# Weight sums by accumulating DMAs, and plain products in the first block alone: an RWKV layer and a feed-forward layer on one core

## The chip, the core and the metric

The kernel runs on one core of one Trainium2 chip. TensorE (PE) multiplies, VectorE (DVE) and ScalarE (ACT) do elementwise work, GpSimd (POOL) and SyncE (SP) issue DMAs. The metric is the device time of one execution in microseconds; smaller is better. Before the change it is 1259.82 us, the median of three runs from 1258.47 to 1259.84 us.

## What is computed

Input is x, 2048 tokens of 512 numbers, in float32 throughout. Two layers follow one another, each behind a layer norm and with a residual. Cut to what matters:

```python
# layer 1 (RWKV): h is a norm of x, hh is h shifted by one token
k = (h * tm_mk + hh * (1 - tm_mk)) @ Wk.T
v = (h * tm_mv + hh * (1 - tm_mv)) @ Wv.T
r = (h * tm_mr + hh * (1 - tm_mr)) @ Wr.T
x = x + sigmoid(r) * wkv(k, v) @ Wo.T            # "time mix"
kk = (h * cm_mk + hh * (1 - cm_mk)) @ Wkey.T     # h: a second norm, "channel mix"
kv = silu(kk) @ Wval.T
sr = sigmoid((h * cm_mr + hh * (1 - cm_mr)) @ Wcr.T)
x = x + sr * kv
# layer 2: h is a norm of x
gate, up = split(h @ w_gate_up.T)
out = (silu(gate) * up) @ w_down.T
x = x + out
```

Wk, Wv, Wr, Wo and Wcr are 512 x 512; Wkey, Wval, gate, up and down are four such blocks each.

## The kernel before

The 2048 tokens are cut into four blocks of 512 (`NB` = 4). Every product of a block is a 512 x 512 x 512 matrix product, or four of them. Most are computed by a Strassen-Winograd scheme, `unit` (L508): each matrix is cut into 2 x 2 quarters of 256, and seven products of quarters take the place of eight. A product of quarters is four matmul instructions of 128x128 by 128x256, each of which the profile shows as two records. The scheme needs four sums of the weight's quarters (S1 to S4, with S1 = A21+A22, S2 = S1-A11, S3 = A11-A21, S4 = A12-S2) and four of the operand's (T1 to T4). `plain_unit` (L619) is the ordinary product, 32 matmul instructions instead of 28, with no sums. The down product of the last layer applies the scheme twice, so that its weight needs sums of sums.

**Weight sums.** `prepare` (L140) makes the four sums of one weight. It loads the four quarters (256 KB each) on GpSimd's queue, adds them on VectorE in four tensor_tensor instructions, and stores the four sums in DRAM, again on GpSimd's queue. There are 32 such blocks: 21 weights, four for the first level of the down weight (`("d", k)`), seven for the second (`("dd", q)`). `weight` and `down_weight` (L164, L170) load a quarter or a sum into a ring of 12 tiles on SP's queue when a product needs it; for a sum, `need_sums` (L275) first makes sure that its instructions have been put out. The first nine blocks use four tiles of the large pool `q`, the others four of the six tiles of the pool `prep`.

**The order of the work.** PE, DVE and ACT execute exactly in the order in which the Python code issues instructions (`manual_schedule`, L1221). GpSimd's and SP's DMAs are placed by the framework's scheduler. The code interleaves by a plan: after each eight or so records of PE, `tick` (L287) grants VectorE a share of that time (`STEP` 1.72 us), and lets background work (norms, mixes, sums of operands) put out instructions until the share is spent. The preparation of weights is metered by `credit`: it grows by `credit[1]` at each tick, and a step of a `prepare` may go when it is at least 1. After a block's loads, `WAIT` = 5 ticks go by before its first addition. `paced` (L127) ties a load to the last matmul issued, so that it doesn't run ahead.

**The sequence.** Block 0's k product comes first, in halves (`first_block`, L729); then r and v of block 0, k of block 1, the output product of block 0, r and v of block 1. The loop over the blocks (L1248) then runs for each block the gate product (WCR), the next block's output product, four up products (WKEY), the down product (WVAL), and the time mix of the block after next. Layer 2 follows (L1286): gate and up products (WG, WU) in four groups, then the twice-cut down product. `PLAIN` = 2 says that blocks 0 and 1 use `plain_unit` for the products of WK, WV, WR and WO.

**Evictions.** `unit` copies partial results from PSUM on ACT (`snapshot`, L542) and adds others on DVE (`add`, L546). Behind that, each product's `sink` applies the nonlinear function on ACT or DVE.

Of the kernel before, what the change touches and what calls it, by code (L numbers as in the profile page):

```python
# [9 lines left out]
F32 = mybir.dt.float32  # L10
AF = mybir.ActivationFunctionType
ALU = mybir.AluOpType
# [3 lines left out]
P = 128  # L16
# [3 lines left out]
NT = TB // P  # L20
HB = TB // 2
EPS = 1e-5
PLAIN = 2
WAIT = 5
STEP = 1.72
SHARE = 0.88
WARM = 44
# [31 lines left out]
def rwkv_ffn_kernel(  # L59
# [29 lines left out]
    def q_tile(name):  # L89
        return pools["q"].tile([P, 2, HB], F32, tag="q", name=name)  # L90
# [30 lines left out]
    for q in (A11, A12, A22, S1, S2, S3, S4):  # L121
        sources["dd", q] = [wd[q, k] if q < 4 else sums["d", k][q - 4] for k in range(4)]
        sums["dd", q] = scratch(f"dd{q}", 4)

    latest = []

# [10 lines left out]
            raw.append(t)  # L137
        return raw

    def prepare(n, own):  # L140

        raw = []
        for k in range(4):
            t = prep.tile([P, 2, HB], F32, tag="raw", name="raw") if own else q_tile("q")
            paced(nc.gpsimd.dma_start(flat(t), sources[n][k]))
            raw.append(t)
        yield 1
        a11, a12, a22, a21 = raw
        for k, o, i0, i1, op in (
            (0, a22, a21, a22, ALU.add),  # L150
            (2, a21, a11, a21, ALU.subtract),
            (1, a11, a22, a11, ALU.subtract),
            (3, a12, a12, a11, ALU.subtract),
        ):
            tt(o, i0, i1, op)
            nc.gpsimd.dma_start(sums[n][k], flat(o))
            yield

    def ring(src):
        t = wring.tile([P, 2, HB], F32, tag="w", name="w")  # L160
# [81 lines left out]
    preps = deque()  # L242
    credit = [0.0, 0.0]

    def prep_one():
        item = preps[0]
        if item[1] > 0:
            return False
        try:
            if next(item[2]) is not None:  # L250
                item[1] = WAIT
        except StopIteration:
            preps.popleft()
            finished.add(("sums", item[0]))
            if len(preps) > 1 and item[3] > 1:
                begin(preps[1])
            elif preps:
                begin(preps[0])
        return True

    def begin(item):
        if not item[4]:
            item[4] = True
            next(item[2])
            item[1] = WAIT

    def prepare_all(ns, own, depth):
        empty = not preps
        for n in ns:
            preps.append([n, 0, prepare(n, own), depth, False])  # L270
        if empty:
            for item in list(preps)[:depth]:
                begin(item)

    def need_sums(n):  # L275
        while ("sums", n) not in finished:
            begin(preps[0])
            preps[0][1] = 0
            prep_one()

    def due():
        for item in put_off:
# [2 lines left out]
            put_off.popleft()[1]()  # L285

    def tick(length=STEP):  # L287
        for item in preps:
            item[1] -= 1
        slack[0] = max(min(slack[0] + SHARE * length - spent[0], 2.5), -2.5)  # L290
        spent[0] = 0.0
        credit[0] = min(credit[0] + credit[1], 2.0)
        while slack[0] > 0 and (hot or background or preps):
            go = False
            if preps and credit[0] >= 1 and prep_one():
                credit[0] -= 1
                go = True
            elif hot or background:
                go = run_one(False)
            slack[0] -= spent[0]  # L300
            spent[0] = 0.0
            if not go:
                break
# [117 lines left out]
    def shifted_norm(s, h, hT, g, b):  # L421
# [10 lines left out]
        nc.vector.tensor_copy(carry[s], hT[:, :, TB : TB + 1])  # L432
        cost(0)

    def sums_of(B):

        for o, i0, i1 in (T1, B12, B11), (T2, B22, T1), (T4, B21, T2), (T3, B22, B12):
            tt(B[o], B[i0], B[i1], ALU.subtract)
            yield

    live_ops = [0]

# [286 lines left out]
    def first_block():  # L729


        xb = xin.pop(0)
        hT = htp.tile([P, NC, TB + 1], F32, tag="hT", name="hT_a")
        hTs[0, "a"] = hT
        h = tok_tile("h")
        m, B = op_tile("mix")
        ops[0, "k"] = B
        finished.add((0, "k"))
        mhalf = const.tile([P, 4], F32, name="mhalf")
        nc.vector.memset(mhalf, -0.5)  # L740
        cols = []

        def normed(j):
            mv = small.tile([P, 2, 2], F32, tag="mv", name="mv")
            yield from moments(xb[:, 2 * j : 2 * j + 2, :], mv)
            var = small.tile([P, 4], F32, tag="var2", name="var2")
            affine(var, mv)
            two = small.tile([P, 4], F32, tag="two", name="two")
            nc.gpsimd.tensor_tensor(two, var, mhalf, ALU.pow)
            yield  # L750
            for t in range(2):
                cols.append((mv[:, t, 0:1], two[:, t : t + 1]))
                ts(
                    h[:, 2 * j + t, :],
                    xb[:, 2 * j + t, :],
                    mv[:, t, 0:1],
                    two[:, 2 + t : 3 + t],
                    ALU.subtract,
                    ALU.mult,
                )  # L760
                yield

        def mixed(j, other):
            at = slice(j * HB, (j + 1) * HB)
            by_one = slice(j * HB + 1, (j + 1) * HB + 1)
            for c in range(NC):
                pt = bank()
                for t in range(2):
                    nc.tensor.transpose(
                        pt[:, 0, t * P : (t + 1) * P],  # L770
                        h[:, 2 * j + t, c * P : (c + 1) * P],
                        ident,
                    )
                nc.scalar.activation(
                    hT[:, c, by_one],
                    pt[:, 0, :],
                    AF.Identity,
                    bias=vcol(LN1B, c),
                    scale=vcol(LN1G, c),
                )  # L780
                d = m[:, 2 * (c // 2) + j, c % 2, :]
                nc.scalar.activation(d, hT[:, c, at], AF.Copy, scale=onem[:, 0, c : c + 1])  # L782
                stt(d, hT[:, c, by_one], vcol(MK, c), d, ALU.mult, ALU.add)
                next(other, None)

        one, two = normed(0), normed(1)
        for _ in range(3):
            next(one)
        next(two)
        for _ in one:  # L790
            pass
        constants()
        nc.vector.tensor_copy(hT[:, :, 0:1], carry["a"])
        next(two)
        next(two)
        mixed(0, two)
        for _ in two:
            pass

        def second():  # L800
            mixed(1, iter(()))
            tails[0] = residual(0, xb, cols)
            nc.vector.tensor_copy(carry["a"], hT[:, :, TB : TB + 1])
            finished.add("norm0")
            slack[0] = spent[0] = 0.0

        return second

# [255 lines left out]
    def quarter_sums(b, n):  # L1064
        x = quarter_operand(b, n)
        asked.add((b, n))

        def run():
            for o, i0, i1 in (T1, B12, B11), (T2, B22, T1), (T4, B21, T2), ("T3", B22, B12):
                tt(x[o], x[i0], x[i1], ALU.subtract)  # L1070
                yield

        urgent((b, "quarters", n), run())

# [139 lines left out]

    early = [WCR] + [WKEY + g for g in range(4)] + [WVAL + g for g in range(4)]
    late = [n + g for g in range(4) for n in (WG, WU)] + [("dd", A11)]
    late += [("d", k) for k in range(4)] + [("dd", q) for q in (S4, S2, A12, S1, S3, A22)]

    ctx.enter_context(  # L1221
        tc.manual_schedule(
# [4 lines left out]
    for n in "rv":  # L1227
        push_mix(0, n, time_mix(0, n))
    push_residual(0)
    credit[1] = 0.5  # L1230
    k_unit(0)
    prepare_all(early, False, 2)
    xin[1] = load_x(1)
    push("norm1", time_norm(1))
    for n in "krv":
# [8 lines left out]
    push_mix(0, "ck", channel_mix(0, "ck"))  # L1244
    r_unit(1)
    v_unit(1)
    prepare_all([WK, WR, WV, WO] + late, True, 1)
    for b in range(NB):  # L1248
        nxt = b + 2 < NB
        if nxt:  # L1250
# [9 lines left out]
        for g in range(4):  # L1260
            up_unit(b, g)
            if b == 1 and g == 0:
                credit[1] = 0.55
            if g == 0:
                if nxt:
                    push_mix(b + 2, "k", time_mix(b + 2, "k"))
                    push_residual(b + 2)
                    push_mix(b + 2, "r", time_mix(b + 2, "r"))
                if b + 1 < NB:
                    push(f"normb{b + 1}", channel_norm(b + 1))  # L1270
                if nxt:
                    push_mix(b + 2, "v", time_mix(b + 2, "v"))
                if b + 1 < NB:
                    push_mix(b + 1, "cr", channel_mix(b + 1, "cr"))
                    push_mix(b + 1, "ck", channel_mix(b + 1, "ck"))
# [3 lines left out]
        if nxt:  # L1279
            for n, u in (("k", k_unit), ("r", r_unit), ("v", v_unit)):  # L1280
                u(b + 2)
    while preps:
        need_sums(preps[-1][0])
    mixes.close()
    last_room()
    for b in range(NB):  # L1286
# [85 lines left out]
```

## Time and profile before

| | |
|---|---|
| median of three runs | 1259.82 us |
| the profiled execution | 1260.03 us |
| its span, from the first to the last instruction | 1258.2 us |
| granted TensorE clock, mean | 0.997 |
| matmul records on PE | 6572 |
| matmul records of `plain_unit` (L640) | 512 |
| DMAs on SP's queue: w from sum / in_w / dd / d / in_wd | 304 / 256 / 112 / 48 / 36 |
| the same, median us from issue to landing | 3.3 / 3.3 / 3.5 / 3.4 / 3.6 |
| bytes read from and written to HBM | 245.39 MB, 41.94 MB |
| DMA engines, mean rate over the span | 229 GB/s |
| ACT activation with silu, 128x512 (L924) | 631 ns each |
| ACT copy from PSUM, 128x512 (L544) | 584 ns each |

The span is what the profile divides; the execution's own time lies 1.8 us above it. A row of the groups of instructions names the line, the engine, the operation, the tiles it writes and reads, their shape, how often it occurs, the busy time and the mean of one, and then how long the engine sat idle just before it and what ended that. Most elementwise rows carry L363, since one helper (`tt`) issues them all, so they are told apart by their tiles: raw and q are weight quarters, mix, s, t and zT operands, u partial results. In a row of a stretch of time each engine has its busy time and count, and the last three columns are the granted clock, the busy share of the 16 DMA engines, and GB/s.

### The profile page before, as it was taken

To read this page: it belongs to the slowest core of one execution; us is meant where nothing else is said; L and a number is where in the kernel's file an instruction comes from. 1 tells how busy PE (TensorE), PEld (TensorE's weight loads), DVE (VectorE), ACT (ScalarE), POOL (GpSimd) and SP (SyncE) were. 2 spreads that over 40 slices of the span, in tenths; PEclk is the share of its full clock that TensorE was granted. 3 is DMA by queue.
4 is the path that set the end of the run, shared out by engine and by line. 5 is a ranking of instruction groups with operands and counts; after the bars stand their busy time and mean duration, and the time that the engine had idled before them with its cause. 6 is when DMAs were issued, how large, how long until landed. Compare 5 with 4: busy or idle time off the path is not lost.

```text
span 1258.2 us, 18321 instructions
## 1 busy us (share of the span) xinstructions
PE 1240.0 (99%) x6572; PEld 1110.7 (88%) x6572; DVE 777.4 (62%) x1416; ACT 369.0 (29%) x687; POOL 151.3 (12%) x276
## 2 busy tenths in 40 slices
PE   9999999999999999999999999999999999999998
PEld 8888888878888888888888888998899988998898
DVE  5756577567786576743473466565766566564476
ACT  6533252252533433302320222112221223112211
POOL 2222211211222212122220000000000000000000
PEclk9999999999999999999999999999999999999999
DMA  6666777887787777789875654795459854785575
GB/s 205 222 209 232 242 242 255 258 269 243 246 264 243 268 251 244 233 279 332 273 253 183 221 154 144 242 337 175 143 169 301 284 154 146 231 291 165 152 220 199
DMA packets 137960, 288.55 MB, mean 229 GB/s; under 512 B 17296, under 2 KB 18320, under 8 KB 136848
## 3 DMA queue, kind: packets, MB, share of 16 engines
q1 hardware_dynamic: 115424, 215.53, 54.9%
q0 software_dynamic: 21440, 70.27, 15.6%
q10 hardware_dynamic: 1008, 1.59, 0.3%
q8 instruction: 53, 0.87, 0.3%
q14 instruction: 35, 0.29, 0.1%
HBM read 245.39 MB, written 41.94 MB: 228 GB/s over the span
## 4 chain that ended last, share of the span: by engine, by line
PE 93%; ACT 3%; DVE 2%; DMA 1%; issue 1%; POOL 0%; DVEq 0%
PE ps L527 71%; PE ps L1126 14%; PE ps L640 6%; PE ps L414 2%; ACT mix L465 1%; DMA raw<-in_w 1%; DVE u L363 0%; DMA w<-in_w 0%; DVE mix L371 0%; DMA x<-in_x 0%; ACT r L835 0%; ACT e L840 0%; DVE e L371 0%; ACT x L701 0%; ACT mix L782 0%
## 5 line engine op out<-in xcount | busy, mean ns | idle before, releaser
L527 PE MATMUL ps<-zT,w 128*128 128x256 f32 x1792 | 391.4, 379 | 0.0
L527 PEld LDWEIGHTS ps<-zT,w 128*128 128x128 f32 x1792 | 338.7, 190 | 45.4
L527 PE MATMUL ps<-mix,w 128*128 128x256 f32 x1232 | 275.9, 383 | 6.0 <-ACT s L544 6.0
L527 PEld LDWEIGHTS ps<-mix,w 128*128 128x128 f32 x1232 | 235.8, 192 | 40.1 <-ACT s L544 7.6
L363 DVE TENSOR_TENSOR u<-ps,u 128x512 f32<-128x512 f32 x128 | 88.5, 692 | 149.2 <-PE ps L527 144.8
L544 ACT COPY u<-ps 128x512 f32<-128x512 f32 x128 | 74.8, 584 | 319.4 <-PE ps L527 319.4
L527 PE MATMUL ps<-w,s 128*128 128x256 f32 x512 | 114.3, 379 | 0.0
L527 PEld LDWEIGHTS ps<-w,s 128*128 128x128 f32 x512 | 97.0, 190 | 13.1
L1126 PE MATMUL ps<-w,hid 128*128 128x128 f32 x832 | 104.7, 275 | 0.4 <-ACT r L1138 0.4
L1126 PEld LDWEIGHTS ps<-w,hid 128*128 128x128 f32 x832 | 99.5, 192 | 1.1 <-ACT r L1138 0.5
L527 PE MATMUL ps<-w,t 128*128 128x256 f32 x432 | 96.5, 379 | 3.1 <-issue 1.8
L527 PEld LDWEIGHTS ps<-w,t 128*128 128x128 f32 x432 | 81.8, 190 | 14.8 <-issue 2.2
L1126 PE MATMUL ps<-w,quads 128*128 128x128 f32 x704 | 89.5, 276 | 0.4 <-ACT r L1138 0.4
L363 DVE TENSOR_TENSOR s<-ps,s 128x512 f32<-128x512 f32 x64 | 44.2, 690 | 69.0 <-PE ps L527 54.0
L1126 PEld LDWEIGHTS ps<-w,quads 128*128 128x128 f32 x704 | 84.3, 192 | 1.1 <-ACT r L1138 0.5
L640 PE MATMUL ps<-mix,w 128*128 128x256 f32 x384 | 83.8, 379 | 1.1 <-DVE mix L371 1.1
L640 PEld LDWEIGHTS ps<-mix,w 128*128 128x128 f32 x384 | 72.6, 190 | 11.1 <-DVE mix L371 1.5
L363 DVE TENSOR_TENSOR u<-u,u 128x512 f32<-128x512 f32 x64 | 44.0, 688 | 51.7 <-ACT u L544 51.7
L1138 ACT COPY r<-ps 128x128 f32<-128x128 f32 x112 | 29.6, 264 | 142.7 <-PE ps L1126 142.7
L363 DVE TENSOR_TENSOR raw<-raw 128x512 f32<-128x512 f32 x92 | 63.2, 687 | 12.0 <-DMA raw<-d 4.5
L1208 POOL DMA_DIRECT2D out<-resid x12 | 8.6, 717 | 469.9 <-DVE resid L363 469.9
L363 DVE TENSOR_TENSOR hid<-hid 128x512 f32<-128x512 f32 x84 | 56.6, 687 | 1.1
(127 smaller groups left out, 1179.4 us busy)
## 6 DMA issues: line engine op xcount, KB each, us to landing
w<-sum SPq DMA_DIRECT2D x304, 256.0 KB, 3.3
w<-in_w SPq DMA_DIRECT2D x256, 256.0 KB, 3.3
w<-dd SPq DMA_DIRECT2D x112, 256.0 KB, 3.5
raw<-in_w POOLq DMA_DIRECT2D x48, 256.0 KB, 4.9
sum<-raw POOLq DMA_DIRECT2D x48, 256.0 KB, 3.9
w<-d SPq DMA_DIRECT2D x48, 256.0 KB, 3.4
q<-in_w POOLq DMA_DIRECT2D x36, 256.0 KB, 6.0
sum<-q POOLq DMA_DIRECT2D x36, 256.0 KB, 3.5
```

What stands on the lines that cost most here:

```text
L363: nc.vector.tensor_tensor(out, a, b, op)
L414: nc.tensor.transpose(flat[:, t * P : (t + 1) * P], h[:, t, c * P : (c + 1) * P], ident)
L465: nc.scalar.activation(dst(c), hT[:, c, 0:TB].rearrange("p (j t) -> p j t", j=2), AF.Copy, scale=onem[:, row - MK, c : c + 1],)
L527: mm = nc.tensor.matmul(pz[:, m, :], lhsT=lhsT, rhs=rhs, start=first and g == 0 and m == 0 and k == 0, stop=g == last and k == 1, skip_gro ...
L544: nc.scalar.copy(tmp[name], acc["z"])
L640: mm = nc.tensor.matmul(acc[i, j][:, m, :], lhsT=act[:, k, lo] if by_token else wg[:, k, lo], rhs=wg[:, k, :] if by_token else act[:, k, : ...
L1126: mm = nc.tensor.matmul(dst, lhsT=x[k][:, g, :], rhs=wt[:, g, :], start=first and g == 0, stop=g == 3, skip_group_check=True,)
L1138: nc.scalar.copy(st["r"][:, m, n * P : (n + 1) * P], st["z"])
L1208: eng.dma_start(out_t[b][:, 2 * j : 2 * j + 2, i * HB : (i + 1) * HB], rs[b][:, 2 * j : 2 * j + 2, i * HB : (i + 1) * HB],)
```

## The change

It does three things.

1. `prepare` no longer adds on VectorE. It takes two tiles instead of four, loads A21 and A22 into them, multiplies both by -1 on ACT, and then makes each sum by a DMA on GpSimd's queue that adds its source to the tile (`accum_op`): t2 = -A22, plus t1 (-A21) gives -S1; t1 plus A11 gives S3; t2 plus A11 gives -S2; t2 plus A12 gives S4. After each, the tile is stored. Only additions occur, so S1 and S2 change their sign, and the operand sums T1, T2 and T4 are formed to match (`sums_in`): T2 by a scalar_tensor_tensor in the place of a tensor_tensor.
2. The two calls of `prepare_all` with their own depths become one queue of 32 blocks, in the order WK, WR, WV, WCR, WO, WKEY, WVAL, WG and WU, d, dd. Up to `DEPTH` = 3 are under way at once (`flying`), in turns. The first three begin in `second`, halfway through the first product. Steps of the preparation no longer count against VectorE's share in `tick`; they go at 2.4 a tick, and at 1.0 from the second block's first up product on, where it was 0.5 and then 0.55.
3. `PLAIN` is 1: in block 1 the products of WK, WR, WV and WO are units of seven products.

```diff
-PLAIN = 2
+PLAIN = 1
 WAIT = 5
+DEPTH = 3
...
+    AFTER = {("dd", q): [("d", k) for k in range(4)] for q in (S1, S2, S3, S4)}
...
-    def prepare(n, own):
-
-        raw = []
-        for k in range(4):
-            t = prep.tile([P, 2, HB], F32, tag="raw", name="raw") if own else q_tile("q")
-            paced(nc.gpsimd.dma_start(flat(t), sources[n][k]))
-            raw.append(t)
+    def prepare(n):
+
+        a11, a12, a22, a21 = sources[n]
+        t1, t2 = prep_tile(), prep_tile()
+        for t, src in (t1, a21), (t2, a22):
+            paced(nc.gpsimd.dma_start(t, src))
         yield 1
-        a11, a12, a22, a21 = raw
-        for k, o, i0, i1, op in (
-            (0, a22, a21, a22, ALU.add),
-            (2, a21, a11, a21, ALU.subtract),
-            (1, a11, a22, a11, ALU.subtract),
-            (3, a12, a12, a11, ALU.subtract),
-        ):
-            tt(o, i0, i1, op)
-            nc.gpsimd.dma_start(sums[n][k], flat(o))
+        for t in t1, t2:
+            nc.scalar.activation(t, t, AF.Copy, scale=-1.0)
             yield
+
+        def add(t, src, k):
+            nc.gpsimd.dma_start(t, src, accum_op=ALU.add)
+            yield
+            nc.gpsimd.dma_start(sums[n][k], t)
+            yield
+
+        yield from add(t2, t1, 0)
+        yield from add(t1, a11, 2)
+        yield from add(t2, a11, 1)
+        yield from add(t2, a12, 3)
...
+    flying = []
+
+    def take():
+
+        while preps and len(flying) < DEPTH:
+            n = preps[0]
+            if n in AFTER and any(("sums", k) not in finished for k in AFTER[n]):
+                return
+            preps.popleft()
+            gen = prepare(n)
+            next(gen)
+            flying.append([n, WAIT, gen])
+
+    def prep_step(item):
+        flying.remove(item)
+        try:
+            next(item[2])
+            flying.append(item)
+        except StopIteration:
+            finished.add(("sums", item[0]))
...
     def prep_one():
+        take()
+        for item in flying:
+            if item[1] <= 0:
+                prep_step(item)
+                return True
+        return False
...
-        credit[0] = min(credit[0] + credit[1], 2.0)
-        while slack[0] > 0 and (hot or background or preps):
-            go = False
-            if preps and credit[0] >= 1 and prep_one():
-                credit[0] -= 1
-                go = True
-            elif hot or background:
-                go = run_one(False)
+        credit[0] = min(credit[0] + credit[1], 4.0)
+        while credit[0] >= 1 and prep_one():
+            credit[0] -= 1
+        while slack[0] > 0 and (hot or background):
+            go = run_one(False)
...
+    def sums_in(B, t3):
+        tt(B[T1], B[B11], B[B12], ALU.subtract)
+        yield
+        stt(B[T2], B[B22], -1.0, B[T1], ALU.mult, ALU.subtract)
+        yield
+        tt(B[T4], B[B21], B[T2], ALU.add)
+        yield
+        tt(B[t3], B[B22], B[B12], ALU.subtract)
+        yield
...
             slack[0] = spent[0] = 0.0
+            take()
+            credit[1] = 2.4
...
-    credit[1] = 0.5
     k_unit(0)
-    prepare_all(early, False, 2)
...
-    prepare_all([WK, WR, WV, WO] + late, True, 1)
...
             if b == 1 and g == 0:
-                credit[1] = 0.55
+                credit[1] = 1.0
```

More of the change, by code (lines that the diff above doesn't have):

```diff
@@ L138, in raw_quarters, with prep_tile @@
         return raw
-    def prepare(n, own):
-        raw = []
-        for k in range(4):
-            t = prep.tile([P, 2, HB], F32, tag="raw", name="raw") if own else q_tile("q")
-            paced(nc.gpsimd.dma_start(flat(t), sources[n][k]))
-            raw.append(t)
-        yield 1
-        a11, a12, a22, a21 = raw
-        for k, o, i0, i1, op in (
-            (0, a22, a21, a22, ALU.add),
-            (2, a21, a11, a21, ALU.subtract),
-            (1, a11, a22, a11, ALU.subtract),
-            (3, a12, a12, a11, ALU.subtract),
-        ):
-            tt(o, i0, i1, op)
-            nc.gpsimd.dma_start(sums[n][k], flat(o))
-            yield
+    def prepare(n):
[3 more added lines that the diff above has]
+            paced(nc.gpsimd.dma_start(t, src))
+        yield 1
+        for t in t1, t2:
+            nc.scalar.activation(t, t, AF.Copy, scale=-1.0)
+            yield
+        def add(t, src, k):
[7 more added lines that the diff above has]
+        yield from add(t2, a12, 3)
+    def prep_tile():
+        return prep.tile([P, 2 * HB], F32, tag="raw", name="raw")
     def ring(src):
@@ L243, in rwkv_ffn_kernel @@
     credit = [0.0, 0.0]
-    def prep_one():
[L246 to L273, printed above, removed]
+    flying = []
[15 more added lines that the diff above has]
+            finished.add(("sums", item[0]))
+    def prep_one():
+        take()
[4 more added lines that the diff above has]
+        return False
     def need_sums(n):
         while ("sums", n) not in finished:
-            begin(preps[0])
-            preps[0][1] = 0
-            prep_one()
+            take()
+            prep_step(next((item for item in flying if item[0] == n), flying[0]))
     def due():
@@ L287, in tick @@
     def tick(length=STEP):
-        for item in preps:
+        for item in flying:
             item[1] -= 1
@@ L433, in shifted_norm @@
         cost(0)
+    def sums_in(B, t3):
[7 more added lines that the diff above has]
+        yield
     def sums_of(B):
-        for o, i0, i1 in (T1, B12, B11), (T2, B22, T1), (T4, B21, T2), (T3, B22, B12):
-            tt(B[o], B[i0], B[i1], ALU.subtract)
-            yield
+        yield from sums_in(B, T3)
     live_ops = [0]
@@ L805, in second @@
             slack[0] = spent[0] = 0.0
+            take()
+            credit[1] = 2.4
         return second
@@ L1068, in run @@
         def run():
-            for o, i0, i1 in (T1, B12, B11), (T2, B22, T1), (T4, B21, T2), ("T3", B22, B12):
-                tt(x[o], x[i0], x[i1], ALU.subtract)
-                yield
+            yield from sums_in(x, "T3")
         urgent((b, "quarters", n), run())
@@ L1213, in ffn_down @@
         down_product(b, sink, final)
-    early = [WCR] + [WKEY + g for g in range(4)] + [WVAL + g for g in range(4)]
-    late = [n + g for g in range(4) for n in (WG, WU)] + [("dd", A11)]
-    late += [("d", k) for k in range(4)] + [("dd", q) for q in (S4, S2, A12, S1, S3, A22)]
+    preps.extend([WK, WR, WV, WCR, WO] + [n + g for n in (WKEY, WVAL) for g in range(4)])
+    preps.extend(n + g for g in range(4) for n in (WG, WU))
+    preps.extend([("d", k) for k in range(4)])
+    preps.extend(("dd", q) for q in (A11, A12, A22, S1, S2, S3, S4))
     ctx.enter_context(
@@ L1281, in rwkv_ffn_kernel @@
                 u(b + 2)
-    while preps:
-        need_sums(preps[-1][0])
+    while preps or flying:
+        need_sums(preps[-1] if preps else flying[-1][0])
     mixes.close()
```

## The prediction

> **What bounds the kernel now.** I read the busy shares first, then the chain of waits, then PE's own list of waits, and last the DMA views, because the change lives on GpSimd's queue.
>
> ```profile
> PE 1240.0 (99%) x6572; PEld 1110.7 (88%) x6572; DVE 777.4 (62%) x1416; ACT 369.0 (29%) x687; POOL 151.3 (12%) x276
> PE 93%; ACT 3%; DVE 2%; DMA 1%; issue 1%; POOL 0%; DVEq 0%
> 157.18 56.98 PE ps L527 x264
> PE ps L527 <- ACT s L544: 6.0, 3, 2.3
> PE ps L414 <- DVE h L367: 1.4, 2, 0.7
> ```
>
> PE is busy for 1240.0 of 1258.2 us and makes 93% of the chain. The third line is one piece of that chain: 264 matmul records without a gap in 56.98 us, so 0.2158 us a record. The fourth and fifth are the largest waits that PE shows after the start, and they come to a few microseconds. Two things only can move the time: fewer records on PE, or something that makes PE wait. VectorE's 62% holds nothing up.
>
> The DMA side has to be read as well:
>
> ```profile
> q0 software_dynamic: 21440, 70.27, 15.6%
> ...
> raw<-in_w POOLq DMA_DIRECT2D x48, 256.0 KB, 4.9
> sum<-raw POOLq DMA_DIRECT2D x48, 256.0 KB, 3.9
> ...
> raw<-in_wd POOLq DMA_DIRECT2D x28, 256.0 KB, 5.1
> ```
> ```profile
> L145 POOL DMA_DIRECT2D raw<-in_w x48 | 26.1, 549 | 44.2 <-PE ps L527 36.7 <-DMA sum<-raw 5.0 <-issue 2.5
> ...
> L363 DVE TENSOR_TENSOR raw<-raw 128x512 f32<-128x512 f32 x92 | 63.2, 687 | 12.0 <-DMA raw<-d 4.5 <-DMA raw<-in_w 4.4 <-issue 1.1
> ```
> ```profile
> 20.00:302.00 282.00, 277.02 (x1305) 243.07 (x1304) 190.68 (x367) 115.25 (x195) 63.90 (x116) 0.99 0.73 239
> ```
> ```profile
> GB/s 0 0 0 0 0 27 75 20 75 259 416 396 410 410 389 403 403 406 373 394 316 328 410 382 376 430 376 396 403 410 382 382 403 362 376 369 369 376 410 403
> ```
>
> A load on POOL's queue lands 4.9 us after its issue, a store 3.9 us, and the issue itself takes 0.55 us. GpSimd's queue used 15.6% of 16 engines for 268 DMAs: 0.156 x 1258.2 / 268 = 0.73 us of all sixteen for each 256 KB. In the window from 20 to 302 us the DMA engines were 73% busy at 239 GB/s. The last line is the first 12 us, where nothing but loads runs: about 395 GB/s is the most that this trace sustains.
>
> **The change, part by part.**
>
> *Fewer matmuls.* With PLAIN at 1, the four units K, R, V and O of block 1 (each 32 matmuls, 64 records) become units of seven products (28 matmuls, 56 records). That takes 4 x 8 = 32 records from PE: 32 x 0.2158 = **-6.9 us**, all of it on the path. The built order agrees: 3,388 matmuls stand where 3,404 stood. The other engines' share has cover: SP gets 3 x 4 = 12 more loads of 256 KB, ACT 12 more copies (0.58 us each), VectorE 32 more adds; all three are far below PE's load.
>
> *Sums leave VectorE.* 32 blocks x 4 tensor_tensor x 0.687 = 88 us go, 32 x 0.69 = 22 us come with the new units. VectorE loses 66 us of 777, worth nothing while PE is the bound. The operand sums (one scalar_tensor_tensor for one tensor_tensor, 0.69 both) cost nothing. But the planner (tick) no longer charges the sums to VectorE, so the norm of block 1 is put earlier: PE's four-way transposes at L414 now stand after 56 instead of 68 plain matmuls, 24 records or 5.2 us sooner. PE waited 1.4 us there for h. I put **+4 us**, from 0 to +7.
>
> *Negations on ACT.* 64 activations of 128x512, nearest row the plain 630 ns one: 40 us on an engine with 29% load. Their length is hidden. Their **wait** is not: each waits for a load on POOL's queue, and behind it in ACT's order stand the copies (L544) that empty PSUM. If the load is late, ACT stops, then PE. Before, this wait was VectorE's, with 11 us in all in the row of L363.
>
> *The pace.* This is the step that decides. In the order before, the 32 blocks' sums are spread from PE's 40 us to its 637 us (the 32 last stores stand that far apart): 19 us a block. In the new order the 320 DMAs stand between 20 and 302 us of PE's work, **8.8 us a block**, because credit is 2.4 per tick until the second channel mix. SP's loads wait for the stores too, but the ring of 12 tiles is 12 x 8 x 0.2158 = 20.7 us deep, and the first use of the gate weights is only at 666 us; ACT's wait comes first.
>
> Can POOL's queue do it in 8.8? For one block the tile t2 goes through load, negation, add, store, add, store, add, store, each waiting for the landing of the one before. With a for an add's landing: 4.9 + 0.7 + 3a + 3 x 3.9 = 17.3 + 3a, shared by three blocks under way. The add is not in this trace. From below: a store's uncrowded minimum in the list of sum is 2.3 us, and one as fast as that would make the chain shorter than 8.8. From above: the rule below, or 6.0, the q loads. **The nearest row** is the load, same queue, same bytes, HBM to SBUF (96 of 128 adds read HBM): a = 4.9. The chain is then 32 us, 10.7 a block, if the three overlapped perfectly. They don't: POOL issues in order, and an issue that waits holds the other blocks back. Walking down POOL's order as built (an issue starts when the one before is issued and what it needs has landed): loads at 0 to 2.8, adds at 6.2, 11.6 and 12.2, the three first stores 11.1, 16.5 and 17.1, and so on; the third block's last store lands at 42.3. Carried on to the end of the order it is 443 us, **13.8 a block**; the last block's second load lands at 410.
>
> From 20 us on, that is 430 us. The negation of this tile stands in ACT's order behind a copy that PE reaches at about 290 us unstalled (gate unit of block 1). PE does not stop the moment ACT does: a unit takes three PSUM banks (z, v, x) of eight in its 12 us, so PE can run on for between 0 and some 25 us; I take 15. **430 - 290 - 15 = +125 us** of stall, spread in steps of 2 to 20 us from about 70 us on.
>
> *A rule against it.* The row says that an add costs what a load costs. The Trainium skill, "Collectives: The Full Stack", section "The bandwidth ceiling: the fold count and why AG ≠ RS ≠ AR", says that an add in the DMA engines reads two sources, two read descriptors a chunk, and so runs at half the rate of a copy. No run here shows an add yet. By it an add holds the sixteen engines for 2 x 0.73 us, so a = 5.6 as an estimate: the walk gives 15.0 a block, its last load 32 us later, stall +157. I take the row, since a quarter of the adds read SBUF and the queue's fixed latency makes most of 4.9, and keep the rule for the range.
>
> *Issue cost* of an add: 0.55, at most double; POOL waits for landings most of the time, so it adds some 5 us at most; taken as 0.
>
> **Sum**, against the profiled execution's span of 1258.2: -6.9 + 4 + 125 = 1380; that execution took 1260.0, 0.2 above the median of 1259.8. With the terms that overlap (the wait of the norm lies ahead of the first stall and gives POOL time), I say **1378 us**.
>
> **Rivals.**
>
> 1. *POOL's chain is late, adds near a load's landing*: 1340 to 1415, 1378 likeliest. For it: 8.8 against 10.7 even with perfect overlap. Chance 0.52.
>
> 2. *The DMA engines are the bound.* In the fast stretch SP moves 43 MB, POOL's plain DMAs 49 and the adds 34: 125 MB, at 395 GB/s 317 us for what is ordered into 282; with the second read of the adds 159 MB, 402 us. Bandwidth alone gives +35 to +120, but on top, landings then grow over 4.9 and 3.9, which were measured at 239 to 262 GB/s. With a = 6.4 the walk gives 16.4 a block: stall about +195, 1450. Chance 0.20. Against it: a stalled PE asks for fewer weights.
>
> 3. *Adds land sooner than loads*, a near 3.9: 12.3 a block, last load 45 us earlier, stall +80; with shorter stores still less. 1275 to 1340, say 1320. Chance 0.17.
>
> 4. *The cover holds: faster.* If an add and a store both land in about 2.6 us, the walk gives 8.5 a block, POOL keeps to the order, ACT never waits, and the 32 records come off: 1259.8 - 6.9 = 1253, or 1257 with the wait at the transposes. The point from which it decides: an add and a store together under about 5.5 us, while the stores alone are at 3.9. Chance 0.08, and 0.03 for a result within the bound of no change. That the records do not go is excluded by the built order.
>
> **How the numbers follow.** Changes under 0.2% (2.5 us) can't be told from none. Slower: 0.52 + 0.20 + 0.17 = 0.89; faster 0.08; same 0.03. The range 1285 to 1470 leaves out rival 4 and no change (0.11), the lowest of 3 and the tail of 2.
>
> **What would show it.** Right: POOL's DMAs up to the last weight sum end past 400 us instead of near 300; PE's waits for ACT total over 80 us between 70 and 450 us; ACT's negations wait for "DMA raw"; PE after that stretch is as before. The landing of raw<-raw and raw<-in_w adds settles a. Wrong: adds that land in under 3 us, or negations that don't wait. If PE's records are fewer by other than 32, the first step fails; if PE waits for "w<-sum" rather than for ACT, the place of the wait does.

## The result, and the profile after

The changed kernel takes **1455.72 us** (median, from 1453.33 to 1457.02), the kernel before 1259.83 us in the same comparison: a ratio of 1.1551, 95% interval 1.1529 to 1.1573. It is 196 us slower. The profiled execution took 1455.54 us, its span is 1453.6 us.

The first fence is the page of the changed kernel: busy time of the engines, the shares of the chain that ended last, and GpSimd's DMA queue (packets, MB, share of 16 engines).

```profile
PE 1281.2 (88%) x6540; PEld 1132.3 (78%) x6540; DVE 718.4 (49%) x1320; ACT 410.5 (28%) x763; POOL 233.3 (16%) x340
...
q0 software_dynamic: 34752, 87.05, 24.3%
...
PE 65%; DMA 26%; issue 3%; POOL 3%; ACT 2%; DVE 1%; POOLq 0%; DVEq 0%; ACTq 0%
```

PE's records fell from 6572 to 6540, the 32 that the change takes away. Yet PE is idle for 1453.6 - 1281.2 = 172.4 us where it was idle for 18.2, and DMAs now make 26% of the chain where they made 1%. The rest of the loss is in PE's busy time itself: it rose by 41.2 us although 6.9 us of work went, so the records that are left took 48 us longer (the last section looks at why). 154.2 + 41.2 is the whole difference of the spans, 195.4 us.

Where it happens is seen in stretches of the traces; the columns are those described above the prediction (granted clock, DMA share and GB/s come last). First the kernel before, then two stretches of the changed kernel.

```profile
20.00:500.00 480.00, 471.52 (x2224) 413.75 (x2223) 331.43 (x631) 191.27 (x319) 105.08 (x192) 1.00 0.75 245
```
```profile
20.00:500.00 480.00, 320.71 (x1291) 266.90 (x1289) 177.71 (x343) 157.21 (x271) 207.47 (x299) 0.81 0.93 251
500.00:1453.00 953.00, 943.31 (x5152) 849.99 (x5152) 531.51 (x948) 244.39 (x476) 19.64 (x28) 0.99 0.64 192
```

From 500 us on PE is 99% busy, as before. Nearly all is lost between 20 and 500 us: 1291 records, where the kernel before has 2224 in the same 480 us. In that stretch the DMA engines are 93% busy where they were 75%, and still move only 251 GB/s where they moved 245.

What PE waits for, and what ACT waits for, in the changed kernel (us in total, times, longest us):

```profile
PE ps L538 <- ACT u L555: 102.0, 12, 19.8
PE ps L538 <- issue: 24.7, 4, 10.8
```
```profile
ACT raw L150 <- DMA raw<-in_w: 109.0, 23, 11.8
...
ACT raw L150 <- DMA raw<-in_wd: 72.1, 12, 11.1
...
ACT raw L150 <- DMA raw<-d: 34.1, 6, 10.7
```

L555 is the copy of a partial result from PSUM (L544 before), L150 the negation of a weight quarter. PE waits for the copy; the copy stands behind a negation in ACT's order; the negation waits for its load. One such place, ACT first and then PE, with the idle time ahead of an instruction in brackets:

```profile
345.51 0.63 ACT L150 ACTIVATE raw<-raw 128x512 f32<-128x512 f32 x1 [10.79 <-DMA raw<-in_wd]
352.28 0.63 ACT L150 ACTIVATE raw<-raw 128x512 f32<-128x512 f32 x1 [6.14 <-DMA raw<-in_wd]
355.22 0.63 ACT L150 ACTIVATE raw<-raw 128x512 f32<-128x512 f32 x1 [2.31 <-DMA raw<-in_wd]
365.75 0.63 ACT L150 ACTIVATE raw<-raw 128x512 f32<-128x512 f32 x1 [9.90 <-DMA raw<-in_wd]
366.28 0.57 ACT L555 COPY u<-ps 128x512 f32<-128x512 f32 x1
```
```profile
366.90 3.45 PE L538 MATMUL ps<-w,s 128*128 128x256 f32 x8 [19.81 <-ACT u L555]
```

Four negations in a row wait 29.1 us for their loads. The copy at 366.28 stands behind them, and PE, which stopped at 347.1, goes on 0.05 us after that copy ends. The four quarters belong to the down weight, whose sums are first loaded at 974 us.

ACT's order holds PE up in a second way: it also makes part of the operands (mix, L476). PE's gap of 10.80 us up to 165.60, for which the profile names no releaser, ends just after such an operand is done, and its part on ACT stood behind a negation that had waited 11.00 us.

The last view is of the instructions of `prepare` in the changed kernel, by line: L154 the accumulating DMAs, L156 the stores. The first two lines belong to the list of the tile raw, the others each end the list of one line.

```profile
L150 ACT ACTIVATE raw<-raw x64: 612/629/638, 32.2 to 500.3; 128x512 f32<-128x512 f32 x64
...
L156 POOL DMA_DIRECT2D dd<-raw x28: 539/561/694, 416.3 to 534.8; - x28
```
```profile
L154 POOL DMA_DIRECT2D raw<-in_w x63: 851/910/1550, 40.0 to 367.2; - x63
...
DMA to landing us min/median/max: 3.3/6.0/9.4
```
```profile
DMA to landing us min/median/max: 2.3/4.4/7.8
```

An add lands 6.0 us after its issue (3.3 at the least), a store 4.4 us (it was 3.9), and the issue of an add takes 0.91 us where a load's takes 0.55. The last store is issued at 534.8 us instead of near 300. Put these landings (6.0, 4.4, and 5.1 for loads) into the prediction's walk down GpSimd's order and it gives 519 us; from the first load, at 16.5 us, to the landing of the last store, at 539, the trace has 523. So the order of the queue and the landings account for the length; why the landings are what they are is the question of the experiments.

### The profile page after: what moved, and what is told of

It is laid out like the page before. It is cut to its first block, busy times and chain, and to the rows that moved or that the text cites. A ratio compares the mean times of both kernels' runs of the same rounds, so it can differ in the third digit from the quotient of the medians.

```text
span 1453.6 us, 18208 instructions
## 1 busy us (share of the span) xinstructions
PE 1281.2 (88%) x6540; PEld 1132.3 (78%) x6540; DVE 718.4 (49%) x1320; ACT 410.5 (28%) x763; POOL 233.3 (16%) x340
## 3 DMA queue, kind: packets, MB, share of 16 engines
q0 software_dynamic: 34752, 87.05, 24.3%
## 4 chain that ended last, share of the span: by engine, by line
PE 65%; DMA 26%; issue 3%; POOL 3%; ACT 2%; DVE 1%; POOLq 0%; DVEq 0%; ACTq 0%
PE ps L538 51%; PE ps L1137 12%; DMA raw<-in_w 10%; DMA raw<-raw 6%; DMA sum<-raw 4%; DMA raw<-in_wd 4%; DMA dd<-raw 1%; POOL raw L154 1%; POOL sum L156 1%; PE ps L417 1%; DMA d<-raw 1%; DMA raw<-d 1%; POOL raw L147 0%; ACT mix L476 0%; PE ps L651 0%
## 5 line engine op out<-in xcount | busy, mean ns | idle before, releaser
L538 PE MATMUL ps<-mix,w 128*128 128x256 f32 x1400 | 339.2, 403 | 89.7 <-ACT u L555 60.6
L538 PEld LDWEIGHTS ps<-mix,w 128*128 128x128 f32 x1400 | 282.8, 204 | 138.1 <-ACT u L555 63.4
L366 DVE TENSOR_TENSOR u<-ps,u 128x512 f32<-128x512 f32 x136 | 94.0, 691 | 181.7 <-PE ps L538 179.0
L555 ACT COPY u<-ps 128x512 f32<-128x512 f32 x136 | 79.2, 583 | 286.9 <-PE ps L538 286.8
L538 PE MATMUL ps<-w,t 128*128 128x256 f32 x456 | 106.2, 389 | 14.4 <-issue 8.4
L538 PEld LDWEIGHTS ps<-w,t 128*128 128x128 f32 x456 | 88.3, 195 | 28.6 <-issue 9.1
L150 ACT ACTIVATE raw<-raw 128x512 f32<-128x512 f32 x64 | 39.6, 627 | 235.3 <-DMA raw<-in_w 109.0
L538 PE MATMUL ps<-w,mix 128*128 128x256 f32 x224 | 58.0, 411 | 22.5 <-issue 16.3
L538 PEld LDWEIGHTS ps<-w,mix 128*128 128x128 f32 x224 | 46.0, 208 | 31.7 <-issue 17.4
L156 POOL DMA_DIRECT2D sum<-raw x84 | 49.1, 584 | 132.8 <-DMA raw<-in_w 95.4
```

Source lines behind the costliest of these rows:

```text
L150: nc.scalar.activation(t, t, AF.Copy, scale=-1.0)
L156: nc.gpsimd.dma_start(sums[n][k], t)
L366: nc.vector.tensor_tensor(out, a, b, op)
L538: mm = nc.tensor.matmul(pz[:, m, :], lhsT=lhsT, rhs=rhs, start=first and g == 0 and m == 0 and k == 0, stop=g == last and k == 1, skip_gro ...
L555: nc.scalar.copy(tmp[name], acc["z"])
```

## The experiments

Two theories of the slow preparation were set against each other: the **chain** (landing times in a row, shared by three blocks) and the **full engines** (the adds fill the 16 DMA engines, and landings grow with what is in flight). Beside them stood two questions: how the lateness reaches PE, and what the other part of the change, PLAIN = 1, is worth. Two of the ten runs are medians of six executions and have a ratio; the other eight are one execution each, so a few microseconds between them mean little.

### Block 1 back to plain products

```diff
-PLAIN = 1
+PLAIN = 2
```

> The changed kernel with PLAIN back at 2, so that block 1's K, R, V and O are plain products again (32 more matmul records on PE, 6.9 us of work). Chain theory (the preparation on GpSimd's queue sets the pace up to its end near 535 us, PE is stretched to it): PE's 6.9 us more lie in the shadow of the stalls, so the time stays within 6 us of the changed kernel, 1450 to 1461 us, and the preparation ends within 15 us of 535. Rival (the stalls come from the sums of WK, WR, WV and WO, needed in block 1 at 60 to 120 us in the changed kernel): without that early need a good part of the stalls goes, 1400 us or less.

1449.3 us; the last store is issued at 517.7 us, 17 earlier than in the changed kernel. Both lie just outside the chain's words and far from the rival's. The 32 records are back and the time is not longer, 6 us shorter if anything; why the preparation got shorter was not followed up. In a stretch that GpSimd's queue paces, 6.9 us of PE's work are worth nothing. The early need of the four weights is not what stalls.

### No negations

```diff
-        for t in t1, t2:
-            nc.scalar.activation(t, t, AF.Copy, scale=-1.0)
-            yield
```

> The changed kernel without the 64 negations on ACT (leaves out the sign of A21 and A22, so S1 to S4 are other sums). Theory (ACT's in-order wait for the loads is what carries the preparation's lateness to PE): 13 blocks alone have an early deadline, the last needed at PE's 194 us; at 16.2 us a block less 0.6 for the negation they are done at about 20 + 13 x 15.6 = 223 us, so PE stalls by some 30 us instead of 215: 1275 to 1310 us, while the preparation still ends at 480 us or later. Rival (the DMA engines are full and PE starves for weights on SP's queue however ACT behaves): over 1380 us, with PE's waits ending on w.

1291.5 us. The preparation is as long as ever (its last store is issued at 526.6 us), the engines as full, and still 164 of the 196 us are gone. PE now waits mostly for early sums, by its list of waits in this run, whose next row is 5.9 us:

```profile
PE ps L534 <- DMA w<-sum: 23.8, 4, 11.0
```

So a late preparation costs little by itself. It was ACT's order that carried into PE's first 500 us the lateness of blocks whose sums were needed much later.

### Five blocks under way

```diff
-DEPTH = 3
+DEPTH = 5
-    prep = mixes.enter_context(tc.tile_pool(name="prep", bufs=6))
+    prep = mixes.enter_context(tc.tile_pool(name="prep", bufs=10))
-    pools = {"q": mixes.enter_context(tc.tile_pool(name="qp", bufs=30))}
+    pools = {"q": mixes.enter_context(tc.tile_pool(name="qp", bufs=26))}
```

> The changed kernel with five blocks under way instead of three (ten tiles of prep, four fewer of q). Chain theory (the landing times in a row bound a block, three share the chain): five share it, about 35 us / 5 = 7 us plus the queue's order, 10 to 12 us a block, the preparation ends near 350 to 400 us and the time falls to 1310 to 1350 us. Rival (the 16 DMA engines are full in that stretch, 93% busy by the profile): landings grow with the number under way, the preparation still takes over 470 us, the time stays over 1410 us.

1408.9 us, a microsecond outside the rival's words and far from the chain's. The list of L154 in this run ends with

```profile
DMA to landing us min/median/max: 3.3/7.2/12.9
```

With five under way an add lands in 7.2 us for 6.0, a store in 5.5 for 4.4, and the preparation ends 46 us sooner (488.6), not 150. The engines were 97% busy from 20 to 455 us. More in flight mostly waits longer: the full engines leave little to gain, and the chain takes what they leave.

### Copies in place of adds

```diff
-            nc.gpsimd.dma_start(t, src, accum_op=ALU.add)
+            nc.gpsimd.dma_start(t, src)
```

> The changed kernel with its 128 accumulating DMAs made plain copies of the same source to the same tile (leaves out the additions). Chain theory: a copy lands in 5.0 to 5.2 us where an add took 6.0, the walk gives 14.6 to 14.9 us a block for 16.2, 41 to 51 us less: 1400 to 1420 us. Rival (full engines, an add holds them twice as long as a copy): the engines' work in the stretch from 20 to 500 us falls from 446 to some 345 us, landings of stores and loads fall too, 1330 to 1375 us.

1389.3 us, between the two. GpSimd's queue on this run's page:

```profile
q0 software_dynamic: 26560, 87.05, 18.4%
```

The same 87.05 MB and 332 DMAs took 0.184 x 1387.3 = 255 us of all sixteen engines; with adds it was 0.243 x 1453.6 = 353 us. That is 98 us for 128 adds, 0.77 us each on top of the 0.77 us that a copy takes: **an add costs the engines about twice a copy** (in the other runs with these adds the queue took 334 to 353 us, which makes it 1.8 to 2.0 times). A copy here landed in 4.7 us and a store in 4.0 (the chain had expected 5.0 to 5.2 and an unchanged store); with both the walk gives 437 us, where the trace has 455 from the first load, at 16.4, to the landing of the last store, at 471. The two theories are one: fuller engines lengthen each landing, and the chain adds the landings up.

### Negations on GpSimd

```diff
-            nc.scalar.activation(t, t, AF.Copy, scale=-1.0)
+            nc.gpsimd.tensor_scalar(t, t, -1.0, None, ALU.mult)
```

> The changed kernel with the 64 negations moved from ACT to GpSimd, where they stand in the same queue as the loads that they wait for. Theory (ACT's order carried the lateness to PE): as in the run without negations PE waits for the early sums alone, with a chain longer by one operation of about 1 us a tile: 1285 to 1320 us, preparation to 530 us or later. Rival (the negations themselves, or the queue's head standing still for them, cost as much as ACT's waits): over 1400 us.

1295.1 us, with the last store issued at 569.4 us. By the list of the tile raw in this run a negation takes GpSimd 1.7 us, and the queue is longer by it:

```profile
L150 POOL TENSOR_SCALAR raw<-raw x64: 1477/1718/2498, 19.9 to 537.6; 128x512 f32<-128x512 f32 x64
```

The preparation got 35 us longer and the kernel 161 us shorter. This computes the same as the changed kernel, so the finding without negations does not hang on what that run left out.

### The same with nine early blocks instead of thirteen

PLAIN = 2 on top, and the blocks in the old order:

```diff
-PLAIN = 1
+PLAIN = 2
-    preps.extend([WK, WR, WV, WCR, WO] + [n + g for n in (WKEY, WVAL) for g in range(4)])
-    preps.extend(n + g for g in range(4) for n in (WG, WU))
+    preps.extend([WCR] + [WKEY + g for g in range(4)] + [WVAL + g for g in range(4)])
+    preps.extend([WK, WR, WV, WO] + [n + g for g in range(4) for n in (WG, WU)])
```

> As the run before, with PLAIN = 2 and the blocks in the old order (WCR, WKEY and WVAL first, then WK, WR, WV, WO). Theory (what counts is blocks due against 16 to 17 us a block): nine blocks are due by PE's 201 us and take 20 + 9 x 16.5 = 169 us, the next four are due at 235 to 289 and take to 235, so PE waits for no sum and the time is that of the kernel before, 1255 to 1268 us, although the engines stay full to about 540 us. Rival (full DMA engines also delay PE's own weight loads): 1285 us or more, waits on w<-in_w.

1264.5 us against 1258.0, a ratio of 1.0048 (1.0028 to 1.0067). Two stretches of this run:

```profile
0.00:55.00 55.00, 50.08 (x245) 44.01 (x246) 31.14 (x83) 34.35 (x61) 28.83 (x39) 0.97 0.85 247
55.00:270.00 215.00, 214.60 (x1017) 188.46 (x1015) 116.80 (x222) 79.43 (x133) 123.30 (x147) 1.00 0.97 278
```

The DMA engines are 97% busy for 215 us and PE is 99.8% busy beside them: full engines alone did not hold PE up here. The loss that remains lies mostly in the first 60 us, where PE gets 268 records done for 283 before, about 3 us: block 1's norm is planned earlier, PE's transposes wait 2.4 us for h where they waited 1.4, and the granted clock is 0.83 from 40 to 50 us where it was 1.00.

### VectorE's sums with PLAIN = 1

The kernel before, with four more blocks in front and an earlier start:

```diff
-PLAIN = 2
+PLAIN = 1
-    early = [WCR] + [WKEY + g for g in range(4)] + [WVAL + g for g in range(4)]
+    early = [WK, WR, WV, WCR, WO] + [WKEY + g for g in range(4)] + [WVAL + g for g in range(4)]
...
+            credit[1] = 0.8
+            prepare_all(early, False, 2)
```

> The kernel before with PLAIN = 1 alone, its sums on VectorE, the preparation begun in the first product in the order WK, WR, WV, WCR, WO, WKEY, WVAL and at 0.8 credits a tick. If the lost 6.9 us of the change hang on the accumulating DMAs alone, this gains them: 1250 to 1256 us. Rival (13 blocks by PE's 194 us are 52 additions of 0.69 us, 36 us, where VectorE already has the first norms to do, so PE waits for VectorE): 1263 to 1282 us, with PE's waits on h and mix before 150 us.

1290.5 us, slower than the rival allowed. PE waits 9.4 us once for h, 13.9 us with no releaser shown and 9.5 us for ACT, and runs at 0.90 of its clock from 60 to 180 us. The old way of adding can't meet thirteen early blocks either, at this start and pace; others were not tried.

### The pace alone

PLAIN = 2 and the old order of blocks as above, the negations on ACT, and

```diff
-            credit[1] = 2.4
+            credit[1] = 1.1
-                credit[1] = 1.0
+                credit[1] = 1.2
```

> The changed kernel with PLAIN = 2, the old order of blocks, negations on ACT, and the pace cut to that of before: 1.1 and then 1.2 credits a tick for 11 steps, some 17 us a block. Theory of the order's pace alone (8.8 us a block was too fast): with 17 us a block asked for and 16 needed the stalls go, 1258 to 1275 us. Rival (the pace is only half of it: a load can't go before the last store of an earlier block has landed, and its negation follows 5 ticks, 8.6 us, later in ACT's order, less than issue, store and load take): ACT still waits, 1300 to 1345 us.

1371.1 us, above even the rival's range. ACT's negations still wait 178.5 us. Here is GpSimd's queue of this run, up to the loads for which ACT waited 18.18 us (until 205.60):

```profile
188.28 0.89 POOL L154 DMA_DIRECT2D raw<-in_w  x1 [3.03 <-issue]
190.23 0.56 POOL L156 DMA_DIRECT2D sum<-raw  x1 [1.06 <-DMA raw<-in_w]
190.87 0.88 POOL L154 DMA_DIRECT2D raw<-in_w  x1
194.76 0.56 POOL L156 DMA_DIRECT2D sum<-raw  x1 [3.02 <-DMA raw<-in_w]
197.29 0.54 POOL L156 DMA_DIRECT2D sum<-raw  x1 [1.97 <-DMA raw<-in_w]
197.95 0.89 POOL L154 DMA_DIRECT2D raw<-in_w  x1
202.04 0.56 POOL L156 DMA_DIRECT2D sum<-raw  x1 [3.19 <-DMA raw<-in_w]
202.58 1.09 POOL L147 DMA_DIRECT2D raw<-in_w  x2
```

ACT had nothing else from 187.4 us on. Its load (L147) is issued at 202.58 only, behind adds and stores of other blocks that each waited 1 to 3 us for a landing. Five ticks cover a load's 5 us, not the queue ahead of it. The slower pace with the old order gained 78 us over PLAIN = 2 alone (1449 us), not the 190 that theory had; a longer WAIT was not tried.

### Negations on VectorE

```diff
-            nc.scalar.activation(t, t, AF.Copy, scale=-1.0)
+            ts(t, t, -1.0, None, ALU.mult)
```

> The changed kernel with the negations on VectorE instead of ACT, the engine that has 88 us of additions less to do. Theory (an engine that PE depends on must not wait in order for GpSimd's queue, whichever it is): the same stall by way of VectorE, 1420 to 1480 us, negations waiting for the loads. Rival (ACT was special, by its load or its PSUM copies): VectorE has room, 1330 us or less.

1449.1 us. The waits of VectorE in this run:

```profile
DVE raw L370 <- DMA raw<-in_w: 110.6, 25, 14.7
```

It is the same stall on the other engine, though the negation takes 0.43 us there; PE's longest row of waits is now 43.7 us for h, which VectorE makes. It is the waiting in order that costs, wherever PE's results pass.

### Ten early blocks, as far as the margin seemed to go

Negations on GpSimd, and of block 1 only WO's product as a unit:

```diff
+UNITS = (WO,)
...
-        plain = b < PLAIN and n <= WO
+        plain = n <= WO and (b < PLAIN or b == 1 and n not in UNITS)
...
-            slack[0] = spent[0] = 0.0
+            slack[0], spent[0] = -2.5, 2.5
```

> Negations on GpSimd, and of block 1 the output product (WO) alone as a unit of seven products, with WCR and WO first in the order of the blocks, and the planner told of 4 us of VectorE time at the start of the preparation, so that the norm of block 1 is put later. Theory: ten blocks are due by PE's 201 us and take 20 + 10 x 16.5 = 185 us, no wait for sums; 8 records less are 1.7 us, and the 3 us lost before 60 us in the run with nine blocks come back: 1254 to 1261 us, within 0.3% of the kernel before on either side. Rival (the full DMA engines cost PE a few microseconds all along): 1262 to 1268 us, as the run with nine blocks.

1273.7 us, ratio 1.0100 (1.0078 to 1.0121), outside both ranges. The planner was told of 2.5 us in this run, not of the 4 us that the expectation names. It did not bring the first 60 us back: PE gets 266 records done there, for 268 with nine blocks. Most of the loss is one wait of PE:

```profile
PE ps L539 <- DMA w<-sum: 12.3, 1, 12.3
```

PE reaches the last of the early sums at 204 us and gets it at 216. 16.5 us a block was the price with PE stalling; beside a PE at full rate, which loads its weights meanwhile, ten blocks took some 19 us each (from the start at 17 us to the issue of the load of that sum at 209.9). One block more than nine was one too many here, and no version tried beats the kernel before.

## Why the prediction was right, and where its sizes were off

The direction, the mechanism and the place held: the result lies in the stated range and 78 us above the single value. Of the signs named, the records fell by 32, POOL's last store was issued at 534.8 us, and PE's waits put down to ACT come to 104 us between 70 and 450 us. But the size was not that of the favoured rival: 1456 us lies above its 1340 to 1415, at the 1450 of the full engines, which had a chance of 0.20. That the range held is owed to its width.

- **Fewer records, -6.9 us.** The records went. The gain did not come, as PLAIN = 2 in the changed kernel showed: the saved work lay in the shadow of the stalls, so the sum should not have counted it.
- **Earlier norm, +4 us.** The run with nine early blocks shows it nearly alone, at about 3 us, of which some 1 us is the wait and most of the rest the lower clock behind it.
- **Negations on ACT hidden in length, not in wait.** Right, and the runs without them on ACT (1291 and 1295 us) make it the largest single piece.
- **POOL can't do 8.8 us a block.** Right. The mis-sized term is the landing. The nearest row was taken for an add, a = 4.9, with stores at 3.9; measured were 6.0 and 4.4, the walk 519 us for 443, the last negation at 500 us for a predicted 430. 500 - 290 = 210 us of lateness, and with -6.9, +4 and the 15 us of running on this leads to 1450 for a span of 1453.6; that it comes so near is in part luck, since the -6.9 was not gained and the 15 was not measured.
- **The rule against it.** The Trainium skill's statement ("Collectives: The Full Stack", "The bandwidth ceiling: the fold count and why AG ≠ RS ≠ AR") that an adding transfer runs at half the rate of a copy, which it makes of ReduceScatter beside AllGather, was the better guide: 1.53 us of all engines for an add, 0.77 for a copy. The estimate of a from it, 5.6, was short of 6.0; with the engines at 93% landings grew, a store's too, from 3.9 to 4.4. The reasons given for preferring the row did not carry: the adds that read SBUF landed in 5.5 us, also above 4.9. How much of a landing is fixed latency no run here shows.
- **The rivals.** The full engines had 1450 us with adds at 6.4 us; they were not a rival but the other half of the same thing. That full engines starve PE of its own loads did not show: at 97% PE was 99.8% busy. Sooner landings and cover that holds are ruled out by the 6.0.

## What to carry to other kernels

An operation that waits for a slow, in-order queue belongs on that queue or on an engine that nobody needs; on ACT, which empties PSUM, its lateness became PE's, even for results that were due 600 us later, and on VectorE as well. Before work is moved to DMAs, price a block twice, by the landings in a row and by the engines' time, at the traffic that the change itself will make, and count how many blocks are due by when. Work saved on an engine in a stretch that something else paces is worth nothing there.

## What the hardware showed beyond that

PE's clock follows its gaps. These are three stretches of 4 us of the changed kernel, after a wait of PE of 7.87 us that ended at 190.68:

```profile
190.00:194.00 4.00, 3.32 (x8) 2.72 (x9) 3.08 (x5) 0.00 (x0) 2.87 (x4) 0.50 0.60 131
194.00:198.00 4.00, 4.00 (x16) 3.38 (x15) 0.00 (x0) 1.11 (x2) 0.58 (x1) 0.77 1.09 214
198.00:202.00 4.00, 4.00 (x20) 3.51 (x20) 0.69 (x1) 0.00 (x0) 3.12 (x5) 1.00 0.89 287
```

For some microseconds after a gap the granted clock is 0.50, and 8 records take nearly the time of 16. The Trainium skill ("TensorE: Matmul & The Clock Gate", "What's actually happening") says much the same: half rate after an idle window of about 3.4 us, full rate after a busy one. Shorter gaps were enough in the run with nine early blocks: after two of 1.7 and 0.7 us, 0.7 us apart, its clock was 0.50 from 45 to 47 us. In the changed kernel the mean over the 480 us is 0.81. A record takes 320.71 / 1291 = 0.248 us there, for 471.52 / 2224 = 0.212 before; over 1291 records that is 47 us, nearly all of the 48 by which the records grew. No run held the clock up during the stalls, so how much of the 196 us it makes on its own stays open; GpSimd's chain accounts for the length of that stretch without it.
